# Layer 0 of a four-layer network: images in pairs, one block's planes by halves, another layout of the columns, a new order of steps

## The chip, the cores and the metric

The kernel runs on one core of a Trainium2 chip, as one program. The metric is the device time of one execution in microseconds (us), the median of several runs. The engines named below are TensorE (PE in the profile), VectorE (DVE), ScalarE (ACT), GpSimd (POOL) and SyncE (SP), which issues nearly all DMAs.

## The reference

Four layers run one after the other on a tensor of 32 images of 96 channels and 56 x 56 points, all in float32. Only layer 0 is touched by the change (layer 2 shares a helper with it). Each layer normalises its input over groups of channels (GroupNorm), computes something of it and adds the input back. Layer 0, for one image:

```
xn  = group_norm(x)                              # per image, over groups of channels
h   = silu(bn1(w_exp @ xn))                      # 96 -> 576 channels, 1x1
h   = silu(bn2(depthwise_3x3(h, w_dw)))          # 576 channels
s   = silu(w_se1 @ mean(h) + b_se1)              # 576 -> 24
h   = h * sigmoid(w_se2 @ s + b_se2)             # 24 -> 576, one gate for each channel
y   = x + xn + bn3(w_proj @ h)                   # 576 -> 96, 1x1
```

## The kernel before, in words

**Tiles.** The 96 channels lie on partitions. An image is stored in `xt` as 224 rows of 14 words (`[C, H * NPH, W4]`): each row of 56 points is split into four column phases (point 4q + p has phase p), because layers 1 and 3 want the image so. Three such buffers turn over. The 576 channels of the middle make four and a half blocks of 128. Blocks 0, 1 and 2 (k = 0..2) have their 3x3 convolution on DVE, block 3 ("ab") and the half block 4 ("c", its 64 channels twice on the partitions, one copy for even and one for odd quarters of the image) have it on PE, as nine matmuls with diagonal weights over a padded plane `hpad`.

**Steps.** `run_steps` (L115) goes once through a string `L0_ORDER` (L58 to 63) for each image n and emits the named steps; a suffix + means image n+1, - means n-1, -- means n-2. PE, DVE and ACT run in exactly this order. SP's queue is ordered by the scheduler. The letters:

- s, q: sums of x and of its squared deviation over the image, each one ACTIVATE over 96 x 3136 with an accumulator (L264). u, v: the sum over the group, a small matmul (L270). m, w, b: mean, deviation (POOL's power), bias.
- n: writes the normalised image `xn` with four ACTIVATEs, one for each column phase (L292). `xn` holds even and odd columns apart. r: the residual x + xn, in place in `xt` (L301).
- e k i: expand, block k, quarter i of the image (14 rows): two matmuls of 392 columns, even and odd columns in two PSUM banks, and one eviction by ACT with the first silu into `hpad` (L313). Three PSUM buffers of two banks each ("mm") turn over.
- f k: the first tap of the convolution (ACT, L321); t k 1..8: the other taps (DVE, L326), 24 for an image. z k: second silu (ACT, L332).
- a i (four) and c i (two): the convolutions on PE, `quarters` (L349), with the silu's eviction into `hab` and `hc`.
- g0 to g4: totals (DVE), squeeze (PE, then ACT), excite (PE), gates (DVE, then ACT), gated (DVE): `wg`, the weights of the projection times the gates.
- p i: project, quarter i: for each of two PSUM banks five matmuls, three with `h2` (L407), one with `hab` (L409), one with `hc` (L410). d i: bn and add into `xt` (DVE, L415).
- o: store: statistics of the result for the next layer (eight bn_stats and an aggregate on DVE, L88), six DMAs of the image to DRAM (L425), the fetch of image b+3 into the buffer that comes free (L196), and some copies that prepare layers 1 and 3 ("asides": `twav`, `tdiff`, on SP's queue).

In `project`, bank j holds columns of parity j of the 14 rows, in the order of the rows. `h2` is read with every second column:

```
out = ps[:C, j, :NT]
for k in range(DV):
    nc.tensor.matmul(out.rearrange("c (r w) -> c r w", w=W2), wg[:, k, :],
                     im["h2"][k][:, rows, j::2], start=(k == 0), stop=False)
```

A store writes 3,584 pieces of 56 bytes (14 words) with each of its six DMAs.

Of the kernel before, what the change touches and what calls it, by code (L numbers as in the profile page):

```python
# [10 lines left out]
F32 = mybir.dt.float32  # L11
BF16 = mybir.dt.bfloat16
# [3 lines left out]
ALU = mybir.AluOpType  # L16
# [9 lines left out]
RT = 7  # L26
# [5 lines left out]
PH = HH * NPH  # L32
NP = H // (2 * RT)
PITCH = W + 1
NPAD = (H + 2) * PITCH + 2
PAIRS = C // 2
GR = 16
HALO = 4
# [21 lines left out]
MANUAL = {mybir.EngineType.PE, mybir.EngineType.DVE, mybir.EngineType.Activation}  # L60
MANUAL_SP = MANUAL | {mybir.EngineType.SP}
L0_ORDER = """
    e00 e01 e02 e03 z0- f0 a3- z2- c1- e10 e11 t01 t02 g0- e12 t03 e30 e40 g1- s+ e13 t04 g2- g3-
    e31 e32 t05 e33 g4- t06 t07 u+ f1 m+ t11 p0- p1- q+ t08 d0- v+ w+ p2- t12 e41 d1- p3- d2- t13
    t14 e20 e21 d3- o- b+ t15 e42 t16 e43 e22 e23 f2 a0 t17 t21 a1 n+ t22 t18 t23 t24 t25 t26 t27 r
    z1 t28 c0 a2
"""
L2_ORDER = """
    e00 e10 e11 e12 l3 j0- d0- e01 e20 e02 e21 r u+ e03 e13 j1- m0 e22 d1- e30 m1 e40 v+ j2- d2- e31
# [54 lines left out]
                step[s[0]](image(b), *map(int, s.rstrip("+-")[1:]))  # L124


def padded(pool, nc, n, dtype, name):

    out = []
    for i in range(n):  # L130
        t = pool.tile([128, NPAD], dtype, tag=f"{name}{i}", name=f"{name}{i}")
        nc.gpsimd.memset(t[:, : PITCH + 1], 0.0)
        nc.gpsimd.memset(t[:, PITCH : PITCH * (H + 2) : PITCH], 0.0)
        nc.gpsimd.memset(t[:, PITCH * (H + 1) :], 0.0)
        out.append(t)
    return out

# [12 lines left out]
        nc.sync.dma_start(to, of)  # L150


def tiles(t):

    return t.rearrange("c (t p r) q -> c t p (r q)", t=NP, p=NPH)


def window(t, p, dy, dx, r0, rows):

    at = (r0 + 1 + dy) * PITCH + 1 + dx  # L160
    return t[:p, at : at + rows * PITCH].rearrange("p (r w) -> p r w", w=PITCH)[:, :, 0:W]


@with_exitstack
def layer0(ctx, tc, S, x, w, y0, norm1, tables, aside):

# [20 lines left out]
        return t  # L189

    xs = {}

    def fetch(b):
        if b < B:
            xs[b] = pool.tile([C, H * NPH, W4], F32, tag="xt", name="xt", bufs=3)
            nc.sync.dma_start(xs[b], x[b])  # L196

    fetch(0)
    S.load(nc, w)
# [5 lines left out]
    bse1 = load("l0_bse1", [SEH, 1])  # L205
    wproj = load("l0_wproj", [128, ND + 1, C])
    out4 = load("l0_out", [C, 4])
    fetch(1)
    fetch(2)

    sc, bi = [], []
    for j in range(2):
# [16 lines left out]
    nc.vector.tensor_tensor(bi3, out4[:, 2:3], sc3, ALU.mult)  # L229
    nc.vector.tensor_tensor(bi3, out4[:, 1:2], bi3, ALU.subtract)  # L230

    eye2 = cp.tile([128, HALF], F32, tag="eye2", name="eye2")
    diag = cp.tile([128, 2, 9, HALF], F32, tag="diag", name="diag")
    hpad = padded(cp, nc, 4, F32, "hpad")
    mv_all = cp.tile([C, B, 2], F32, tag="mv0", name="mv0")
    h2s = [cp.tile([128, H, W], F32, tag=f"h2{i}", name=f"h2{i}") for i in range(2)]


    tables()
    nc.vector.tensor_tensor(eye2, S.ident[:, :HALF], S.ident[:, HALF:], ALU.add)  # L240
    for k in (AB, CC):
        for t in range(9):
            nc.vector.tensor_scalar(diag[:, k - AB, t, :], eye2, wdw[:, COL[k], t : t + 1], None, ALU.mult)
    late = ctx.enter_context(tc.tile_pool(name="l0l", bufs=1))
    h2s += [late.tile([128, H, W], F32, tag=f"h2{i}", name=f"h2{i}") for i in (2, 3)]
    hab = late.tile([128, NP, 2, NT], F32, tag="hab", name="hab")
    wg = late.tile([128, ND + 1, C], F32, tag="wg", name="wg")
    h2s.append(late.tile([128, H, W], F32, tag="h24", name="h24"))
    hc = late.tile([128, 2, 2, NT], F32, tag="hc", name="hc")

    ims = {}

    def image(b):

        if b not in ims:
            ims[b] = {
                "b": b, "xt": xs.pop(b), "h2": [None] * DV, "ps": [None] * NP,
                "pad": [hpad[(DV * b + k) % 2] for k in range(DV)] + hpad[2:],
                "ss": sm.tile([128, ND], F32, tag="ss", name="ss"),
            }  # L260
        return ims[b]


    def sums(im, name, func, bias):  # L264
        im[name] = sm.tile([C, 1], F32, tag=name, name=name)
        junk = pool.tile([C, HW], BF16, tag="junk", name="junk", bufs=1)
        nc.scalar.activation(junk, im["xt"].rearrange("c r q -> c (r q)"), func, bias=bias,
                             accum_out=im[name])

    def group_sum(im, name):  # L270
        im["ps" + name] = psm.tile([C, 1], F32, tag="sm", name="pn")
        nc.tensor.matmul(im["ps" + name], S.grp, im[name], start=True, stop=True)

    def mean(im):
        im["nm"] = sm.tile([C, 1], F32, tag="nm", name="nm")
# [16 lines left out]
    def normalise(im):  # L292
        im["xn"] = pool.tile([C, 2, H, W2], F32, tag="xn", name="xn", bufs=1)
        for p in range(NPH):
            nc.scalar.activation(
                im["xn"][:, p % 2].rearrange("c (t r) (q m) -> c m t (r q)", t=NP, m=2)[:, p // 2],
                tiles(im["xt"])[:, :, p], AF.Identity, bias=im["nb"], scale=im["rstd"])

    def residual(im):
# [3 lines left out]
    def expand(im, k, i):  # L303

        c = COL[k]
        rows = slice(2 * i * RT, 2 * (i + 1) * RT)
        ps = psum.tile([128, 2, 512], F32, tag="mm", name="ps")
        for j in range(2):
            nc.tensor.matmul(  # L309
                ps[:, j, :NT], wexp[:, k * 128 : k * 128 + 128],  # L310
                im["xn"][:, j, rows, :].rearrange("c h w -> c (h w)"), start=True, stop=True,
            )
        nc.scalar.activation(  # L313
            window(im["pad"][k], 128, 0, 0, 2 * i * RT, 2 * RT).rearrange("p r (w j) -> p j r w", j=2),
            ps[:, :, :NT].rearrange("p j (r w) -> p j r w", w=W2),
            AF.Silu, bias=bi[0][:, c : c + 1], scale=sc[0][:, c : c + 1],
        )

    def first_tap(im, k):
        im["h2"][k] = h2s[(DV * im["b"] + k) % len(h2s)]  # L320
# [14 lines left out]
    def end_block(im, k):  # L335
        silu2(k, im["h2"][k], im["h2"][k], im["ss"][:, k : k + 1])

    def quarters(k, pad, tiles):


        ps = psum.tile([128, 2, 512], F32, tag="mm", name="psd")
        for t in range(9):
            for j in range(2):
                for r in range(2):
                    c = r ^ j
                    p = slice(r * HALF, (r + 1) * HALF)
                    at = (2 * tiles[r] * RT + t // 3) * PITCH + t % 3
                    v = pad[p, at : at + 2 * RT * PITCH].rearrange("p (r w) -> p r w", w=PITCH)
                    nc.tensor.matmul(  # L349
                        ps[c * HALF : (c + 1) * HALF, j, :NT].rearrange("p (r w) -> p r w", w=W2),  # L350
                        diag[p, k - AB, t, :], v[:, :, j:W:2], start=(t == 0), stop=(t == 8),
                    )
        return ps

# [8 lines left out]
    def depthwise_c(im, i):  # L363

        if i == 0:
            im["hc"] = hc
            im["pc"] = sm.tile([128, 2], F32, tag="pc", name="pc")
        ps = quarters(CC, im["pad"][CC], (2 * i, 2 * i + 1))
        silu2(5, im["hc"][:, i], ps[:, :, :NT], im["pc"][:, i : i + 1])


# [28 lines left out]
    def project(im, i):  # L400
        wg = im["wg"]
        rows = slice(2 * i * RT, 2 * (i + 1) * RT)
        ps = im["ps"][i] = psum.tile([128, 2, 512], F32, tag="mm", name="psj")
        for j in range(2):
            out = ps[:C, j, :NT]
            for k in range(DV):
                nc.tensor.matmul(out.rearrange("c (r w) -> c r w", w=W2), wg[:, k, :],  # L407
                                 im["h2"][k][:, rows, j::2], start=(k == 0), stop=False)
            nc.tensor.matmul(out, wg[:, 3 + j, :], im["hab"][:, i, j, :], start=False, stop=False)  # L409
            nc.tensor.matmul(out, wg[:, 5 + (i % 2 ^ j), :], im["hc"][:, i // 2, j, :], start=False, stop=True)  # L410

    def add(im, i):
        for j in range(2):
            v = tiles(im["xt"])[:, i, j::2]
            nc.vector.scalar_tensor_tensor(  # L415
                v, im["ps"][i][:C, j, :NT].rearrange("c (x m) -> c m x", m=2), sc3, v, ALU.mult, ALU.add)
        if im["b"] == B - 1:
            store_tile(nc, y0, im, i)

    def store(im):  # L420
        b, xt = im["b"], im["xt"]
        channel_stats(nc, sm, xt, mv_all[:, b, :], "t")
        if b < B - 1:
            for to, of in groups(xt, y0, lambda y: y[:, :, b, :], store=True):
                nc.sync.dma_start(to, of)  # L425
        fetch(b + 3)
        if b < B - 4:
            for start in aside[b :: B - 4]:
                start()
        del ims[b]  # L430
# [449 lines left out]
def layer2(ctx, tc, S, k2, y1, y2, norm3):  # L880
# [187 lines left out]
    def store(im):  # L1068
        b = im["b"]
        channel_stats(nc, sm, im["xt"], mv_all[:, b, :], "t")  # L1070
        if b == B - 2:
            for to, of in groups(im["xt"], y2, lambda y: y[:, :, b, :], store=True):
                nc.sync.dma_start(to, of)
        elif b % 2 and b < B - 1:
            for to, of in groups(im["pair"], y2, lambda y: y[:, :, b - 1 : b + 1, :], store=True):
                nc.sync.dma_start(to, of)
            fetch(b + 5)
        del ims[b]

# [289 lines left out]
```

## Time and profile before

| | us |
|---|---|
| median of 3 runs | 6391.51 |
| lowest, highest | 6384.19, 6391.89 |
| the profiled execution | 6501.16 |
| its span | 6499.3 |

The profile describes one execution, and that one was 110 us longer than the median of the runs. The page's first part gives the share of the span for which each engine was busy; layer 0 is about its first half. A few groups of layer 0, from the list of instructions of one round (1800 to 1896 us):

| line | engine, what | count | busy us | mean ns |
|---|---|---|---|---|
| L326 | DVE, tap | 25 | 86.6 | 3480 |
| L349 | PE, depthwise | 432 | 38.5 | 511 |
| L309 | PE, expand | 80 | 27.9 | 497 |
| L313 | ACT, eviction of expand | 20 | 21.4 | 1081 |
| L407 | PE, project with `h2` | 48 | 18.0 | 509 |
| L415 | DVE, add | 8 | 4.6 | 616 |
| L267 | ACT, sums | 2 | 5.7 | 2799, 2909 |

Matmuls overlap in PE's pipeline, so their mean is longer than the distance from one to the next; the busy time is the sum without overlaps. A float32 matmul appears as more than one record.

### The profile page before, as it was taken

The page shows a single profiled execution, that of the slowest core. Times are in us where ns is not written, and L with a number is a line of the kernel's source. Part 1 is how long each engine was busy: PE and PEld are TensorE (multiplying, and loading weights), DVE is VectorE, ACT ScalarE, POOL GpSimd, SP SyncE. Part 2 cuts the span into 40 slices and gives each one's busy share as a digit, 9 for nine tenths or more (in the row PEclk, how much of TensorE's full clock was granted, in tenths as well). Part 3 has the DMA queues.
Part 4 walks back from the last instruction along what each step waited for, and adds up shares of the span by engine and source line. Part 5 has one row for each costly group of instructions (what it writes and reads, how often), then busy time and mean ns, then how long its engine had stood idle before and what let it go on. Part 6 is the DMA issues. An engine that isn't in the chain of part 4 may idle for free.

```text
span 6499.3 us, 115397 instructions
## 1 busy us (share of the span) xinstructions
PE 6025.5 (93%) x49064; PEld 3599.1 (55%) x49064; DVE 5168.3 (80%) x5469; ACT 3953.6 (61%) x5268; POOL 234.1 (4%) x157
## 2 busy tenths in 40 slices
PE   6989989998998998989969999989999999999699
PEld 3444444444444444444535666667777777778344
DVE  8989979898998998989957766657777767676587
ACT  6556555655656565556635565557767766677355
POOL 4000000000000000000000000000000000000000
PEclk8999999999999999989979999999999999999899
DMA  2486475839539439474655776656869695953888
GB/s 80 29 41 50 41 43 41 46 44 40 47 41 41 43 47 42 39 41 39 17 60 143 141 155 150 143 36 45 48 42 50 44 49 41 51 38 31 166 253 248
DMA packets 1631554, 452.94 MB, mean 70 GB/s; under 512 B 1447406, under 2 KB 1625318, under 8 KB 1627582
## 3 DMA queue, kind: packets, MB, share of 16 engines
q1 hardware_dynamic: 1631038, 445.55, 65.7%
q8 instruction: 386, 6.32, 0.6%
q14 instruction: 130, 1.06, 0.1%
HBM read 284.44 MB, written 214.08 MB: 77 GB/s over the span
## 4 chain that ended last, share of the span: by engine, by line
PE 71%; ACT 9%; DMA 9%; SPq 6%; DVE 3%; issue 1%; POOL 1%; ACTq 0%; DVEq 0%
PE psd L349 14%; PE psd L1019 11%; PE ps L309 9%; PE psj L407 8%; PE pc L735 6%; PE ps L1000 5%; SPq L425 4%; DMA y<-xt 4%; PE pc L1175 3%; PE psj L1056 3%; PE psj L409 3%; PE psj L410 2%; ACT hi L972 2%; ACT a L990 2%; DVE h L326 2%; PE pc L719 2%
## 5 line engine op out<-in xcount | busy, mean ns | idle before, releaser
L326 DVE SCALAR_TENSOR_TENSOR h<-hpad,l_wdw,h 128x3136 f32<-128x3136 f32 x768 | 2659.6, 3480 | 28.7 <-ACT h L321 14.9
L349 PE MATMUL psd<-hpad,diag 64*64 64x392 f32 x13824 | 1239.6, 512 | 13.4 <-issue 13.4
L313 ACT ACTIVATE hpad<-ps,o,s 128x784 f32<-128x784 f32 x640 | 684.3, 1081 | 773.3 <-PE ps L309 771.3
L309 PE MATMUL ps<-xn,l_wexp 96*128 96x392 f32 x2560 | 931.6, 516 | 135.6 <-ACT hpad L313 129.1
L1019 PE MATMUL psd<-apad,diag 64*64 64x392 bf16 x20736 | 931.5, 332 | 110.4 <-ACT a L990 57.2
L349 PEld LDWEIGHTS psd<-hpad,diag 64*64 64x64 f32 x13824 | 547.5, 132 | 694.9 <-issue 656.8
L1019 PEld LDWEIGHTS <-diag 64*64 64x64 bf16 x20736 | 695.6, 107 | 342.3 <-issue 164.7
L309 PEld LDWEIGHTS ps<-xn,l_wexp 96*128 96x128 f32 x2560 | 493.4, 197 | 524.2 <-ACT hpad L313 135.3
L565 ACT COPY T<-raw 32x112 f32<-32x112 f32 (+2 forms) x1440 | 462.8, 384 | 308.1 <-DMA raw<-tdiff 223.3
L990 ACT ACTIVATE u<-ps,o,s 128x784 int16<-128x784 f32 x576 | 536.3, 1002 | 162.0 <-PE ps L1000 143.6
L990 ACT ACTIVATE a<-psd,o,s 128x784 int16<-128x784 f32 x448 | 423.7, 999 | 327.7 <-PE psd L1019 327.7
L407 PE MATMUL psj<-h,wg 128*96 128x392 f32 x1536 | 591.4, 520 | 27.9 <-ACT hpad L313 26.4
L1000 PE MATMUL ps<-hi,l_w1q 96*128 96x392 f32 x1280 | 462.4, 361 | 10.0 <-ACT hi L972 9.2
L1175 PE MATMUL pc<-x,T 128*112 128x416 f32 (+1 forms) x1152 | 415.2, 523 | 48.1 <-DMA raw<-tdiff 47.6
L735 PE MATMUL pc<-x,T 128*112 128x416 f32 (+1 forms) x1152 | 445.8, 523 | 0.0
L1000 PE MATMUL ps<-lo,l_w1q 96*128 96x392 f32 x1280 | 438.0, 342 | 0.0
L407 PEld LDWEIGHTS psj<-h,wg 128*96 128x96 f32 x1536 | 249.4, 166 | 289.3 <-issue 258.3
L1175 PEld LDWEIGHTS pc<-x,T 128*112 128x112 f32 x1152 | 204.7, 178 | 258.1 <-issue 240.7
L332 ACT ACTIVATE hab<-psd,o,s 128x392 f32<-128x392 f32 x256 | 170.6, 671 | 263.5 <-PE psd L349 263.5
L332 ACT ACTIVATE h<-h,o,s 128x3136 f32<-128x3136 f32 x96 | 287.9, 2999 | 19.7 <-DVE h L326 19.7
L321 ACT ACTIVATE h<-hpad,l_wdw 128x3136 f32<-128x3136 f32 x96 | 279.1, 2907 | 9.3 <-DMA twav<-zwav 8.3
L735 PEld LDWEIGHTS pc<-x,T 128*112 128x112 f32 x1152 | 190.9, 178 | 143.9 <-issue 143.9
(202 smaller groups left out, 6793.5 us busy)
## 6 DMA issues: line engine op xcount, KB each, us to landing
X<-y SPq DMA_DIRECT2D x192, 392.0 KB
xt<-in_x_dram SPq DMA_DIRECT2D x32, 1176.0 KB
y<-xt SPq DMA_DIRECT2D x192, 196.0 KB
y<-y SPq DMA_DIRECT2D x96, 392.0 KB
xt<-y SPq DMA_DIRECT2D x96, 392.0 KB
out_dram<-y SPq DMA_DIRECT2D x96, 392.0 KB
y<-xt SPq DMA_DIRECT2D x90, 392.0 KB
twav<-zwav SPq DMA_DIRECT2D x768, 36.8 KB
```

Of the source, the lines that this page charges most:

```text
L309: nc.tensor.matmul(ps[:, j, :NT], wexp[:, k * 128 : k * 128 + 128], im["xn"][:, j, rows, :].rearrange("c h w -> c (h w)"), start=True, sto ...
L313: nc.scalar.activation(window(im["pad"][k], 128, 0, 0, 2 * i * RT, 2 * RT).rearrange("p r (w j) -> p j r w", j=2), ps[:, :, :NT].rearrange ...
L326: nc.vector.scalar_tensor_tensor(h2, window(im["pad"][k], 128, t // 3 - 1, t % 3 - 1, 0, H), wdw[:, k, t : t + 1], h2, ALU.mult, ALU.add,)
L332: nc.scalar.activation(view, ps, AF.Silu, bias=bi[1][:, c : c + 1], scale=sc[1][:, c : c + 1], accum_out=accum)
L349: nc.tensor.matmul(ps[c * HALF : (c + 1) * HALF, j, :NT].rearrange("p (r w) -> p r w", w=W2), diag[p, k - AB, t, :], v[:, :, j:W:2], start ...
L407: nc.tensor.matmul(out.rearrange("c (r w) -> c r w", w=W2), wg[:, k, :], im["h2"][k][:, rows, j::2], start=(k == 0), stop=False)
L565: nc.scalar.copy(to.rearrange("x t (p s) -> x t p s", p=NPH), v[:, k])
L735: nc.tensor.matmul(ps[:PH, to], st["T"][j][:, h, k, :], st["x"][:, j, h, of], start=False, stop=(n == NK - 1))
L990: nc.scalar.activation(out, ps, AF.Identity, bias=o[:, c : c + 1], scale=s[:, c : c + 1])
L1000: nc.tensor.matmul(ps[:, j, :NT], w1[:, k * 128 : k * 128 + 128], im[part][:, r0 : r0 + RT, :].rearrange("c h w -> c (h w)"), start=(part ...
L1019: nc.tensor.matmul(ps[q, j, :NT].rearrange("p (r w) -> p r w", w=W), diag[p, k, t, :], v, start=(t == 0), stop=(t == 8))
L1175: nc.tensor.matmul(ps[:, :, to], st["T"][:, h, k, :], st["x"][:, h, :, of], start=(n == 0), stop=(n == NK - 1))
```

## The change

- Images are kept in pairs: two tiles `xt0` and `xt1` of `[C, 224, 2, 14]` take the place of three single ones; an image is a view of one half. The input lies in DRAM in the same pairs. `fetch(b)` is called for even b only and loads images b and b+1; the store of an odd image b calls it for b+3. `store_images` writes images b-1 and b together with six DMAs whose pieces are 112 bytes; images 30 and 31 are still written alone.
- `sums` makes four ACTIVATEs over 96 x 784 into four columns, with a smaller scratch tile, and `group_sum` adds the columns with four accumulating matmuls.
- Block 4's plane `hhalf` has 28 rows: the lower 64 partitions hold rows 0 to 27, the upper ones 28 to 55, each with the neighbour row at the border. Its evictions write 64 partitions, and quarters 1 and 2 have a second, small eviction of one row. Result tile i of c holds quarters i and i + 2.
- Column phases: PSUM bank j of `quarters` and `project` holds phases 2j and 2j+1 (columns 4q + 2j and 4q + 2j + 1). `h2` and the planes are read as pairs of neighbouring words, four words apart. `project` writes its bank with phase 2j first and then phase 2j+1, so that two words that follow each other go to places 196 words apart. `add` then reads the bank straight through and updates 28 rows of 14 words.
- `eye2` lives in `wg`, and the diagonal weights are built after the call of `tables()`.
- A new `L0_ORDER`: step n and e00 to e03, f0 of the next image stand at the end of a round; a3 stands after them; store stands at the start of the second round after its image's (o--, before: o- right behind d3-); s+ is the eighth step of a round.

```diff
-    e00 e01 e02 e03 z0- f0 a3- z2- c1- e10 e11 t01 t02 g0- e12 t03 e30 e40 g1- s+ e13 t04 g2- g3-
-    e31 e32 t05 e33 g4- t06 t07 u+ f1 m+ t11 p0- p1- q+ t08 d0- v+ w+ p2- t12 e41 d1- p3- d2- t13
-    t14 e20 e21 d3- o- b+ t15 e42 t16 e43 e22 e23 f2 a0 t17 t21 a1 n+ t22 t18 t23 t24 t25 t26 t27 r
-    z1 t28 c0 a2
+    z2- c1- o-- t01 g0- e40 g1- s+ t02 e41 e10 e30 g2- e11 t03 u+ g3- e31 e12 t04 e13 g4- f1 t05
+    p0- e32 r t06 m+ q+ p1- t11 d0- t07 d1- t08 z0 t12 p2- d2- p3- e20 t13 d3- v+ w+ e42 e21 e22
+    t14 e23 t15 f2 t16 e33 e43 a0 t21 t17 a1 a2 b+ n+ t22 t23 t18 c0 e00+ e01+ z1 t24 t25 t26 t27
+    e02+ e03+ f0+ a3 t28
...
+def store_images(nc, y, im):
+
+    b = im["b"]
+    if b == B - 2:
+        t, at = im["xt"], b
+    elif b % 2 and b < B - 1:
+        t, at = im["pair"], slice(b - 1, b + 1)
+    else:
+        return
+    for to, of in groups(t, y, lambda y: y[:, :, at, :], store=True):
+        nc.sync.dma_start(to, of)
...
+    pairs = [cp.tile([C, H * NPH, 2, W4], F32, tag="xt0", name="xt0")]
 
     def fetch(b):
+
         if b < B:
-            xs[b] = pool.tile([C, H * NPH, W4], F32, tag="xt", name="xt", bufs=3)
-            nc.sync.dma_start(xs[b], x[b])
+            pair = pairs[b // 2 % 2]
+            nc.sync.dma_start(pair, x[b // 2])
+            for j in range(2):
+                xs[b + j] = pair, pair[:, :, j, :]
...
+    hpad = padded(cp, nc, 3, F32, "hpad") + padded(cp, nc, 1, F32, "hhalf", HH)
...
+        im[name] = sm.tile([C, NP], F32, tag=name, name=name)
+        for i in range(NP):
+            junk = pool.tile([C, 2 * RT * NPH, W4], BF16, tag="junk", name="junk", bufs=1)
+            nc.scalar.activation(junk, im["xt"][:, i * 2 * RT * NPH : (i + 1) * 2 * RT * NPH], func, bias=bias,
+                                 accum_out=im[name][:, i : i + 1])
...
-        nc.tensor.matmul(im["ps" + name], S.grp, im[name], start=True, stop=True)
+        for i in range(NP):
+            nc.tensor.matmul(im["ps" + name], S.grp, im[name][:, i : i + 1], start=(i == 0), stop=(i == NP - 1))
...
+        parts = [(slice(128), 2 * i * RT, slice(2 * RT))]
+        if k == CC:
+            lo, up = slice(64), slice(64, 128)
+            parts = [(up if i // 2 else lo, i % 2 * 2 * RT, slice(2 * RT))]
+            parts += [[], [(up, -1, slice(2 * RT - 1, 2 * RT))], [(lo, HH, slice(1))], []][i]
...
+    def phases(v, j):
+
+        return v.rearrange("p r (q j m) -> p j r q m", j=2, m=2)[:, j]
...
-                        ps[c * HALF : (c + 1) * HALF, j, :NT].rearrange("p (r w) -> p r w", w=W2),
-                        diag[p, k - AB, t, :], v[:, :, j:W:2], start=(t == 0), stop=(t == 8),
+                        ps[c * HALF : (c + 1) * HALF, j, :NT].rearrange("p (r q m) -> p r q m", q=W4, m=2),
+                        diag[p, k - AB, t, :], phases(v[:, :, :W], j), start=(t == 0), stop=(t == 8),
...
-        ps = quarters(CC, im["pad"][CC], (2 * i, 2 * i + 1))
+        ps = quarters(CC, im["pad"][CC], (i, i))
...
-            out = ps[:C, j, :NT]
+            out = ps[:C, j, :NT].rearrange("c (m r q) -> c r q m", m=2, q=W4)
+            hab, hc = (im[n].rearrange("p i j (r q m) -> p i j r q m", q=W4, m=2) for n in ("hab", "hc"))
             for k in range(DV):
-                nc.tensor.matmul(out.rearrange("c (r w) -> c r w", w=W2), wg[:, k, :],
-                                 im["h2"][k][:, rows, j::2], start=(k == 0), stop=False)
-            nc.tensor.matmul(out, wg[:, 3 + j, :], im["hab"][:, i, j, :], start=False, stop=False)
-            nc.tensor.matmul(out, wg[:, 5 + (i % 2 ^ j), :], im["hc"][:, i // 2, j, :], start=False, stop=True)
+                nc.tensor.matmul(out, wg[:, k, :], phases(im["h2"][k][:, rows], j), start=(k == 0), stop=False)
+            nc.tensor.matmul(out, wg[:, 3 + j, :], hab[:, i, j], start=False, stop=False)
+            nc.tensor.matmul(out, wg[:, 5 + (i // 2 ^ j), :], hc[:, i % 2, j], start=False, stop=True)
...
-            v = tiles(im["xt"])[:, i, j::2]
+            n = 2 * i + j
+            v = im["xt"][:, 2 * n * 2 * RT : 2 * (n + 1) * 2 * RT, :]
             nc.vector.scalar_tensor_tensor(
-                v, im["ps"][i][:C, j, :NT].rearrange("c (x m) -> c m x", m=2), sc3, v, ALU.mult, ALU.add)
+                v, im["ps"][i][:C, j, :NT].rearrange("c (r q) -> c r q", q=W4), sc3, v, ALU.mult, ALU.add)
...
-        channel_stats(nc, sm, xt, mv_all[:, b, :], "t")
-        if b < B - 1:
-            for to, of in groups(xt, y0, lambda y: y[:, :, b, :], store=True):
-                nc.sync.dma_start(to, of)
-        fetch(b + 3)
+        b = im["b"]
+        channel_stats(nc, sm, im["xt"], mv_all[:, b, :], "t")
+        store_images(nc, y0, im)
+        if b % 2:
+            fetch(b + 3)
```

## The prediction

> **What bounds the kernel now.** First the slices of the page (40 slices of 162 us). Layer 0 fills the first 20 or so.
>
> ```profile
> PE   6989989998998998989969999989999999999699
> DVE  8989979898998998989957766657777767676587
> ACT  6556555655656565556635565557767766677355
> PEclk8999999999999999989979999999999999999899
> ```
>
> TensorE is the busiest engine there, VectorE (DVE) close behind, ScalarE (ACT) far from full; but both leading engines dip in the same slices. So I listed who waits in 100 to 2900 us (us in total, times, longest):
>
> ```profile
> ACT junk L267 <- DMA xt<-in_x_dram: 138.6, 7, 27.0
> DVE wg L397 <- ACT gate L393: 136.1, 7, 26.6
> PEld ps L309 <- ACT hpad L313: 132.0, 7, 26.6
> PE ps L309 <- ACT hpad L313: 127.0, 7, 26.0
> ```
>
> These are seven events, each seen four times: the sums of image n+1 (step s) wait on ACT for their fetch, the evictions behind them leave TensorE without a free PSUM buffer, and the gates behind those hold DVE. Next, stretches with and without such an event (columns: PE, PEld, DVE, ACT, POOL busy, then clock, DMA share, GB/s):
>
> ```profile
> 1800.00:1896.00 96.00, 94.59 (x620) 47.08 (x619) 92.36 (x52) 61.68 (x63) 3.63 (x1) 1.00 0.36 47
> 1896.00:1992.00 96.00, 94.59 (x620) 47.11 (x619) 92.38 (x52) 61.72 (x63) 3.63 (x1) 1.00 0.60 44
> 1505.00:1620.00 115.00, 92.34 (x601) 45.69 (x600) 89.08 (x48) 62.13 (x62) 1.42 (x1) 0.88 1.38 30
> ```
>
> A clean round is all TensorE: 94.6 of 96 us, and nothing but shorter TensorE work could shorten it. The start of step s in the timeline of ACT goes from 142.8 us (image 2) to 3119.1 us (image 31): 2976.3 us in 29 rounds, mean 102.6, while clean ones take 96.35. The excess is 2976.3 - 29 x 96.35 = 182 us. Last, why a fetch is late, in SP's own timeline (start, duration):
>
> ```profile
> 695.06 30.68 SPq L425 DMA_DIRECT2D y<-xt  x6
> ...
> 735.89 0.32 SPq L196 DMA_DIRECT2D xt<-in_x_dram  x1
> ...
> 793.16 57.21 SPq L425 DMA_DIRECT2D y<-xt  x6
> ...
> 871.15 0.34 SPq L196 DMA_DIRECT2D xt<-in_x_dram  x1
> ```
>
> The fetch reuses the stored buffer, so it waits for the store. Mostly that takes 41 us, but for images 2, 6, 9, 13, 18, 22, 25 and 29 the six stores of 56-byte pieces last 66 to 76 us to the last packet. Layer 2 stores pairs, 112-byte pieces, and each of its 15 stores looks like this one, with 40 to 42 us to the last packet:
>
> ```profile
> 4731.53 33.37 SPq L1076 DMA_DIRECT2D y<-xt  x6
> ```
>
> **What the Trainium skill says.** "DMA: Bandwidth & Descriptors", Specifications, wants at least 512 B per transfer for line rate. The trace agrees in kind: twice the bytes in layer 2's pair store took no longer than a single image's. "TensorE: Matmul & The Clock Gate", What's actually happening, says that an idle window of about 3.4 us halves the clock; the trace shows 0.88 in the stretch with a stall and 1.00 in the clean ones, so a stall costs a little more than its length. "PSUM — Partial Sum Buffer", Specifications, has 8-byte lines and says that any non-contiguous pattern slows matmuls significantly; no row of before writes single words apart. "SBUF — State Buffer", Specifications, wants two hits per 16-byte line; the old stride-2 reads and the new pairs both give two.
>
> **The change, part by part.**
>
> *Pairs.* Stores become 15 of the layer 2 kind and two singles at the end. I take layer 2's 40 to 42 us for all of them, so the slow ones go, and with them up to 182 us. But three single buffers become two pairs: a fetch is issued once in two rounds, in the round whose step s needs it. Two things hold it. The store of the pair begins when step d3- ends. Let P be the end of p3- on TensorE; d3- ends at P+1.4, the last packet is out at about P+45. And the fetch comes after o--'s eight bn_stats, which now stand behind 13 taps: 13 x 3.48 us on DVE brings t28 to P+47.4, and eight bn_stats with the aggregate (3.83 + 0.37) to P+51.6. SP has one aside copy (twav) between store and fetch, no more; behind the waiting fetch stand the copies that prepare layers 1 and 3, for which nothing in layer 0 waits. A single fetch lands 7 us after issue, two queued together at the start of the kernel took 13, so the pair is there at about P+64.7.
>
> When is it wanted? On TensorE after p3-: e20, v+, 6 e, a0 a1 a2, c0, 4 e+, a3. With e at 1.315 us, one depthwise call (quarters) at 6.38, this is about P+47; c1- ends at 53.5, e40 at 54.8. ACT does z2-, c1- and e40 by 56.0, squeeze's silu by 56.4, and then stands at s+. So it waits about 8.3 us. Behind it queue the evictions of e41, e10 and e30; TensorE has three PSUM buffers, fills them, and stops at e11. That is 14 rounds (images 4, 6, ... 30), each 8.3 us plus about 1 us of half clock. With a store that ended later the wait would grow only beyond P+51.6: that is the cover.
>
> *Sums in quarters.* Four ACTIVATEs of 784 (about 1.0 us each from the rows of that size) with an accumulator read of 0.19 for one of 2.80: ACT has room, +1.5 us twice a round. Group sums take four matmuls for one: three more at 0.11 us, twice, 0.7 us of TensorE per round.
>
> *Halves of block 4.* Same number of matmuls. Evictions on 64 partitions are no shorter than on 128; two small ones (64 x 56) add about 0.2 us each on ACT, hidden under TensorE. Memsets and the diagonals, now built later, are in the prologue.
>
> *Column phases, reads.* 432 depthwise and 48 project passes a round read pairs in place of every second word. Stride-2 reads pitch at 345 to 352 ns, contiguous ones at 329. Bounds: 0, or what separates them, 23 ns on each of 108 groups of depthwise matmuls and 16 ns on each of 48 project passes: 3.2 us a round. A loss has no bound from the trace; the skill's two hits per line, which stay, speak against one. I take 0.
>
> *Column phases, writes.* 80 passes of project per image write words 196 apart. Bound below 0: no reason excludes a small gain. Bound above: twice the pass, 80 x 0.33 = 26 us a round. The nearest rows: bf16 passes of 392 pitch at 165 ns, fp32 ones at 329, so a float pass with one word per line would ask for as many PSUM lines per ns as the bf16 one already gets (1.2). I take 0. The add reads PSUM contiguously now: layer 2's does, at 618 ns against 616, so 0.
>
> *Order.* Per round TensorE has 94.8 + 0.7 = 95.5 us of work. Laid out by hand with these durations, it waits 0.8 us for the totals (g0- behind t01 on DVE), 0.6 to 1.3 for e41's eviction behind s+, and about 0.7 elsewhere: 97.6 us (to 98.5), against 96.35. At 95 us of work DVE is just covered.
>
> *Prologue.* The first fetch is two images, image 0 is there 6 us later. The tail stays.
>
> **The sum**, against the profiled execution: 15 rounds x 97.6 + 14 x (97.6 + 9.3) = 1464 + 1497 = 2961; 2961 - 2976 + 6 = -10 us on its 6499.3 us of span. The median of the runs, 6391.5, is 110 us below that execution (6501.2); I carry the difference over as it is: 6381, rounded to 6380. What a measurement of this kernel tells from no change is about 0.2%, 13 us.
>
> **The rivals.** A is this sum: the slow stores are traded for a wait in every other round. Range 6335 (stall 5 us in place of 8.3) to 6430 (rounds of 98.5, stall 10). Chance 0.42: 0.22 faster, 0.10 the same, 0.10 slower.
>
> B, the wait is mostly hidden: the fetch of a pair takes less than 13 us, ACT reaches s+ later than laid out, or pair reads are cheaper (3.2 x 29 = 93 us). With a stall of 2 us: 15 x 97.6 + 14 x 99.8 = 2861, and -109 in all: 6280. For it speaks that the fetch's two parts (7 and 13 us) come from a start with other loads in flight; against it that DVE, full as it is, can't bring o-- forward. Chance 0.26.
>
> C, the scattered PSUM writes cost. At 0.1 us a pass 8 us a round, 6640; at twice the pass 7200. For it speaks the skill's page, against it the line rate. Chance 0.12.
>
> D, slower: the late fetches are to a good part the profiled execution's own. It is 110 us longer than the median, and the 56-byte stores are what varies in it. The gain is the excess that timed runs have; the costs (15 x 1.25 + 14 x 10.55 + 6 = 172 us) stay. It decides from an excess below 172. If all 110 us were missing, 72 would be left: 6391 + 100 = 6490; half of it gives 6435. For it speaks that nothing else in layer 0 varies; against it that layers 1 to 3 move most of the data and may hold the difference. Chance 0.20, of which 0.18 slower.
>
> **How the numbers follow.** Faster: 0.22 + 0.26 = 0.48; the same 0.10 + 0.02; slower 0.10 + 0.18 + 0.12 = 0.40. The likeliest is A, 6380. A range for 8 in 10 takes in A, most of B (to 6265) and D to 6500, and leaves C out.
>
> **What would show it.** In the new trace: pair stores all near 41 us; step s waiting for its fetch 14 times for about 8 us, and in between no wait on a DMA; the project passes' mean unchanged near 510 to 520 ns; rounds alternating between about 98 and 107 us. A mean of project well above 520 is C. Even rounds above 99 mean that the order leaves more holes than I laid out. No waits of s+ mean B.

## The result, and the profile after

The changed kernel takes 6550.06 us (median of 4 runs, 6541.39 to 6563.87), the kernel before 6389.99 us: a ratio of 1.0254, with a 95% interval of 1.0235 to 1.0273. It is 160 us slower. The profiled execution of the changed kernel has a span of 6562.0 us.

First the waits of the changed kernel in 100 to 3000 us (us in total, times, longest):

```profile
ACT junk L287 <- DMA xt<-in_x_dram: 100.3, 13, 8.5
PEld ps L330 <- ACT hhalf L342: 117.8, 28, 9.1
PE ps L330 <- ACT hhalf L342: 115.4, 28, 9.0
DVE wg L431 <- ACT gate L427: 143.5, 28, 10.3
```

The seven long waits for a fetch have become thirteen of about 8 us, in every other round (a fourteenth, of 9.0 us, lies behind this window). Here is one of them, first on SP, then on DVE, then on ACT (start, duration). The step p3- of this round ended at 2176.6 us; this is P.

```profile
2177.84 33.44 SPq L162 DMA_DIRECT2D y<-xt  x6
2227.74 0.34 SPq L211 DMA_DIRECT2D xt<-in_x_dram  x1
```

```profile
2216.95 7.01 DVE L355 SCALAR_TENSOR_TENSOR h<-hpad,l_wdw,h 128x3136 f32<-128x3136 f32 x2
2223.87 3.84 DVE L87 BATCH_NORM_STATS2 stt<-xt 96x6 f32<-96x392 f32 x8
2227.74 0.37 DVE L88 BATCH_NORM_AGGREGATE mv<-stt 96x2 f32<-96x48 f32 x1
```

```profile
2232.81 0.23 ACT L415 ACTIVATE s1g<-pse,l_bse 24x1 f32<-24x1 f32 x1
2240.90 0.86 ACT L287 ACTIVATE junk<-xt 96x784 bf16<-96x784 f32 x1 [7.86 <-DMA xt<-in_x_dram]
```

The fetch goes out at P+51.1, in the moment in which the eight bn_stats end, and not when the pair's store has been issued (P+34.7). ACT is free at P+56.4 and gets the pair at P+64.3.

Second, one short and one long round by the windows view (PE, PEld, DVE, ACT, POOL busy, clock, DMA share, GB/s), and four slices of 4 us in the short one:

```profile
1968.30:2076.90 108.60, 100.24 (x634) 49.94 (x633) 92.54 (x51) 64.94 (x76) 3.63 (x1) 0.92 0.37 67
2076.90:2176.60 99.70, 99.19 (x634) 49.09 (x633) 92.52 (x51) 64.94 (x76) 3.63 (x1) 0.97 0.05 15
2134.90:2138.90 4.00, 3.49 (x19) 2.41 (x18) 3.96 (x4) 3.90 (x9) 0.00 (x0) 1.00 0.00 0
2138.90:2142.90 4.00, 4.00 (x13) 2.60 (x12) 3.50 (x3) 3.37 (x4) 0.00 (x0) 0.52 0.00 0
2142.90:2146.90 4.00, 4.00 (x9) 2.26 (x8) 3.08 (x2) 3.25 (x5) 0.00 (x0) 0.63 0.00 0
2146.90:2150.90 4.00, 4.00 (x13) 2.00 (x12) 3.96 (x2) 3.74 (x3) 0.00 (x0) 1.00 0.00 0
```

TensorE is busy for 99.2 of the short round's 99.7 us and waits for 0.5; clean rounds of before had 94.6 of 96. Part of the difference is the clock: it falls to half at P+62 although TensorE has work. The clock's records in the trace show a half-clock stretch at that place in every one of the 27 rounds that I counted, 324 us of them in all: 6.8 us in 12 of the 14 short rounds and 10.2 in two, 17.1 us in the long ones, where the wait for the pair stands in front of it. TensorE's timeline shows what stands there in the short round:

```profile
2136.58 1.49 PE L420 MATMUL pg<-s1g,l_wse 24*128 24x1 f32 x12
2138.58 2.58 PE L330 MATMUL ps<-xn,l_wexp 96*128 96x392 f32 x4 [0.51 <-ACT hhalf L342]
2140.95 1.33 PE L293 MATMUL pn<-s,grp 96*96 96x1 f32 x8
2142.14 5.04 PE L330 MATMUL ps<-xn,l_wexp 96*128 96x392 f32 x9
```

Excite's twelve one-column records (a matmul shows as two), a wait of half a microsecond, the first four expand passes, eight one-column records of the group sum; and then nine passes of expand in 5.04 us, which take 3 us at full clock.

What the column phases cost is seen in the instructions of the same short round:

```profile
L383 PE MATMUL psd<-hpad,diag 64*64 64x392 f32 x288 | 25.8, 511 | 0.0
L442 PE MATMUL psj<-h,wg 128*96 128x392 f32 x48 | 17.9, 506 | 0.0
L450 DVE SCALAR_TENSOR_TENSOR xt<-psj,sc,xt 96x392 f32<-96x392 f32 x8 | 4.6, 616 | 4.0 <-PE psj L444 4.0
```

Before, the depthwise matmul, project with `h2` and the add took 511, 509 and 616 ns: the phases cost nothing.

### The profile page after: what moved, and what is told of

Same layout as the page of the kernel before. It is cut to its first block, busy times and chain, and to the rows that moved or that the text cites. A ratio compares the mean times of both kernels' runs of the same rounds, so it can differ in the third digit from the quotient of the medians.

```text
span 6562.0 us, 116352 instructions
## 1 busy us (share of the span) xinstructions
PE 6129.5 (93%) x49448; PEld 3678.3 (56%) x49448; DVE 5159.4 (79%) x5469; ACT 4045.6 (62%) x5716; POOL 225.4 (3%) x157
## 4 chain that ended last, share of the span: by engine, by line
PE 72%; DVE 12%; ACT 8%; DMA 5%; issue 1%; POOL 1%; SPq 1%; ACTq 0%; DVEq 0%; POOLq 0%
PE psd L1053 11%; DVE h L355 10%; PE psd L383 10%; PE ps L330 9%; PE psj L442 8%; PE ps L1034 6%; PE pc L769 6%; PE pc L1205 6%; PE psj L1090 3%; DMA xt<-in_x_dram 3%; PE psj L443 3%; PE psj L444 3%; ACT hi L1006 2%; ACT junk L287 2%; PE pc L753 2%; ACT a L1024 2%
## 5 line engine op out<-in xcount | busy, mean ns | idle before, releaser
L330 PE MATMUL ps<-xn,l_wexp 96*128 96x392 f32 x2560 | 1021.5, 551 | 160.3 <-ACT hhalf L342 130.1
L1053 PEld LDWEIGHTS <-diag 64*64 64x64 bf16 x20736 | 713.0, 108 | 340.7 <-issue 176.2
L330 PEld LDWEIGHTS ps<-xn,l_wexp 96*128 96x128 f32 x2560 | 523.4, 211 | 562.8 <-issue 142.5
L342 ACT ACTIVATE hpad<-ps,o,s 128x784 f32<-128x784 f32 x512 | 543.0, 1075 | 463.0 <-PE ps L330 460.3
L383 PE MATMUL psd<-hpad,diag 64*64 64x392 f32 x9216 | 825.5, 511 | 0.0
L383 PEld LDWEIGHTS psd<-hpad,diag 64*64 64x64 f32 x9216 | 353.3, 131 | 461.4 <-issue 461.0
L442 PE MATMUL psj<-h,wg 128*96 128x392 f32 x1536 | 573.4, 508 | 2.7 <-DVE wg L431 1.5
L383 PE MATMUL psd<-hhalf,diag 64*64 64x392 f32 x4608 | 416.5, 509 | 0.0
L1205 PEld LDWEIGHTS pc<-x,T 128*112 128x112 f32 x1152 | 204.7, 178 | 245.8 <-issue 225.4
L383 PEld LDWEIGHTS psd<-hhalf,diag 64*64 64x64 f32 x4608 | 178.3, 131 | 227.0 <-issue 227.0
```

The costliest lines, as they stand in the source:

```text
L330: nc.tensor.matmul(ps[:, j, :NT], wexp[:, k * 128 : k * 128 + 128], im["xn"][:, j, rows, :].rearrange("c h w -> c (h w)"), start=True, sto ...
L342: nc.scalar.activation(window(im["pad"][k][p], p.stop - (p.start or 0), 0, 0, r0, n).rearrange("p r (w j) -> p j r w", j=2), ps[p, :, :NT] ...
L383: nc.tensor.matmul(ps[c * HALF : (c + 1) * HALF, j, :NT].rearrange("p (r q m) -> p r q m", q=W4, m=2), diag[p, k - AB, t, :], phases(v[:, ...
L442: nc.tensor.matmul(out, wg[:, k, :], phases(im["h2"][k][:, rows], j), start=(k == 0), stop=False)
L1053: nc.tensor.matmul(ps[q, j, :NT].rearrange("p (r w) -> p r w", w=W), diag[p, k, t, :], v, start=(t == 0), stop=(t == 8))
L1205: nc.tensor.matmul(ps[:, :, to], st["T"][:, h, k, :], st["x"][:, h, :, of], start=(n == 0), stop=(n == NK - 1))
```

## The experiments

All times below are medians, and each ratio is to the kernel before, run on the same chip with it. The chips were not the same throughout, and the kernel before took 6380 to 6387 us beside the experiments and 6390 beside the changed kernel; so a few microseconds between versions on different chips say nothing.

**The kernel before once more.** No edit. The profile on which I had built the sum was an execution 110 us above the median, so I wanted another one.

> The kernel before, unchanged, for a second profile of it. Theory 1 (its late fetches belong to the kernel): again seven or eight stores of 66 to 76 us, about 180 us of excess over 96.35 us rounds in layer 0, and an execution near 6500. Theory 2 (they belong mostly to that one profiled execution): an execution near 6390 with some 70 to 90 us of excess, three or four late fetches.

Measured: 6389.58 us, ratio 1.0005 (0.9996 to 1.0014); the span of its profiled execution is 6393.5 us. Its waits in 100 to 2900 us:

```profile
ACT junk L267 <- DMA xt<-in_x_dram: 58.0, 7, 9.8
PEld ps L309 <- ACT hpad L313: 51.1, 7, 9.4
PE ps L309 <- ACT hpad L313: 45.6, 7, 8.8
DVE wg L397 <- ACT gate L393: 55.6, 7, 9.4
```

The same seven fetches of the same images are late, but each by less: 4.8 to 9.8 us where the first profile had 11.6 to 27.0. For the store of image 6 and the fetch behind it, SP's timeline has:

```profile
776.27 45.60 SPq L425 DMA_DIRECT2D y<-xt  x6
837.25 0.34 SPq L196 DMA_DIRECT2D xt<-in_x_dram  x1
```

Step s of image 2 to step s of image 31 takes 2881.8 us, which is 88 us above 29 rounds of 96.35, not 182. Theory 2 had the size right and the number of late fetches wrong: the late fetches do belong to the kernel, but more than half of their length (138.6 us against 58.0) belonged to that execution. Its slow stores of 56-byte pieces were longer (57.21 us of issue for image 6 against 45.60 here); why, no run here shows.

**The store earlier.** In the order of the changed kernel the store goes right behind d3-:

```diff
-    z2- c1- o-- t01 g0- e40 ...
+    z2- c1- t01 g0- e40 ...
-    ... e20 t13 d3- v+ w+ ...
+    ... e20 t13 d3- o- v+ w+ ...
```

> The changed kernel with one step moved: the store (bn_stats, then the pair's fetch) stands right behind d3- instead of two rounds' starts later. Theory 1 (the wait for the pair in every other round is made by the eight bn_stats behind 13 taps): the pair lands about P+55 to P+58 in place of P+64, step s waits 0 to 2 us, the long rounds come from 108.6 to about 101, time about 6550 - 14 x 7 = 6450. Rival (the wait is the store's own length and the fetch's): the wait stays at 5 us or more and the time within 40 us of 6550.

Measured: 6443.78 us, ratio 1.0098 (1.0068 to 1.0128), 106 us less than the changed kernel.

```profile
2113.27 33.23 SPq L162 DMA_DIRECT2D y<-xt  x6
2154.31 0.34 SPq L211 DMA_DIRECT2D xt<-in_x_dram  x1
```

The fetch now goes out 41.0 us after the store, when the store has landed, and step s waits at most 1.8 us (6.0 us in all). So the place of the bn_stats made the wait. The rounds, though, are 99.7 to 102 us: the half-clock stretch in every round has stayed.

**Single images, four buffers.** The changed kernel with four single images in place of two pairs, stored as before in 56-byte pieces:

```diff
-            pair = pairs[b // 2 % 2]
-            nc.sync.dma_start(pair, x[b // 2])
+            xs[b] = singles[b % 4]
+            nc.sync.dma_start(xs[b], x[b])
...
-        if b % 2:
-            fetch(b + 3)
+        fetch(b + 4)
```

> The changed kernel with four single image buffers in place of two pairs (56-byte stores again, fetch of image b+4), order as changed. Every fetch then has a round of slack. Theory 1: all rounds near 99.7 us, no wait of step s, 6550 - 14 x 9 = 6425. Rival (56-byte stores disturb by more than late fetches, so that pairs are needed): 6480 or more.

Measured: 6438.23 us, ratio 1.0087 (1.0067 to 1.0107). No fetch is late at all, though the stores are the short-pieced ones, and rounds are 99.7 to 102 us. A round of slack does as much as pairs with an early store; what remains above the kernel before is not the fetch.

**The order of before in the changed kernel.** Only the string is exchanged.

> The changed kernel with the order of steps of before, everything else as changed. If the order is what lost (theory 1: the short rounds are 3.3 us longer because small matmuls stand together and the clock is halved after them, the long ones because of the late store step), rounds go to about 97 to 98 us, time 6390 to 6430. If the pairs, the halves or the column phases lose by themselves (rival), it stays above 6480.

Measured: 6387.74 us, ratio 1.0002 (0.999 to 1.0014). Pairs, halves, split sums and column phases together neither gain nor lose. Inside, they do both: no fetch is late and the 29 rounds take 2868.8 us (13 less than before), but step s of image 2 stands at 160.2 us, where it stood at 143.0 before. And the rounds do not become the clean ones of before, with 96.3 us; here are two:

```profile
1882.20:1981.70 99.50, 97.77 (x634) 48.34 (x633) 92.84 (x52) 64.90 (x76) 3.63 (x1) 0.98 0.40 72
1981.70:2079.40 97.70, 97.48 (x633) 48.27 (x632) 92.73 (x51) 64.98 (x76) 3.63 (x1) 0.98 0.05 16
```

Together the 29 rounds are 75 us above 29 clean ones, so most of the 88 us that the kernel before loses there is lost again in another way. An estimate from this trace covers it: 96 us at half clock, in 24 stretches, cost about 48, and the larger group sums 1.0 us a round (1.5 us of TensorE against 0.5), which is 29. No run takes the two apart.

**The new order in the kernel before.** The reverse: only the string, with three single buffers.

> The kernel before with the new order of steps, nothing else of the change. Its fetch is a single image, issued at P+51 in every round, and lands about P+58.5. Theory 1 (the order is what loses, and pairs make its late store step worse): a wait of step s of 1 to 3 us in every round, the half-clock stretch in every round, rounds of 99 to 101 us, 6400 to 6460: between both kernels. Rival (the order only loses together with the split sums and halves): 6390 or less.

Measured: 6483.4 us, ratio 1.0147 (1.012 to 1.0173): more than I had expected. One short round, one long:

```profile
1931.50:2030.90 99.40, 98.22 (x622) 48.98 (x621) 92.59 (x51) 62.04 (x62) 3.63 (x1) 0.97 0.43 44
2030.90:2140.20 109.30, 99.27 (x622) 49.53 (x621) 92.58 (x51) 61.93 (x62) 3.63 (x1) 0.92 1.00 40
```

Step s waits about 2 us in every round, as expected, and 11 to 14 us where the 56-byte store is slow, which I had left out: the later the fetch, the more a slow store shows. So the order costs 98 us on the old buffers (6386 to 6483) and 162 us on the new ones (6388 to 6550).

**One group-sum matmul.**

```diff
-        im["ps" + name] = psm.tile([C, 1], F32, tag="sm", name="pn")
-        for i in range(NP):
-            nc.tensor.matmul(im["ps" + name], S.grp, im[name][:, i : i + 1], start=(i == 0), stop=(i == NP - 1))
+        pn = psm.tile([C, NP], F32, tag="sm", name="pn")
+        nc.tensor.matmul(pn, S.grp, im[name], start=True, stop=True)
+        im["ps" + name] = sm.tile([C, 1], F32, tag="ps" + name, name="pt")
+        nc.vector.tensor_reduce(im["ps" + name], pn, AX.X, ALU.add)
```

> The changed kernel with one group-sum matmul over four columns in place of four accumulating ones, and a small reduce on DVE behind it. Theory 1 (the four small matmuls cost 1.6 us a round themselves, and the thin stretch on TensorE that they make with squeeze and excite halves the clock for 6.8 us, which costs another 3.4): short rounds go from 99.7 to 97 or 98 and half-clock stretches become fewer than one a round; 6470 to 6510. Rival (thin matmuls only cost their own time): 1.3 us a round, half-clock stretches as before, 6510 to 6520.

Measured: 6523.9 us, ratio 1.0215 (1.0185 to 1.0244): 26 us less than the changed kernel, which misses both forecasts by 4 to 14 us. Short rounds are 97.0 to 98.7 us in place of 99.7, but the start of layer 0 is 12 us longer (step s of image 2 at 169.3 us in place of 157.2), and a half-clock stretch is still there in all 27 rounds, often shorter. Fewer thin matmuls do not take it away.

**One group-sum matmul, with the order of before.** The same edit, and the string of `old_order`.

> The changed kernel with the order of before and one group-sum matmul in place of four: no late fetch, no extra small matmuls. Theory 1: rounds of 96.4 to 97.5 us, 29 x 1.5 us below the version with the old order alone: 6340 to 6360, under both kernels. Rival (what the thin matmuls gave up comes back as the wait of the project on the silu that it already shows in some rounds): 6370 or more.

Measured: 6384.55 us, ratio 1.0003 (0.9991 to 1.0014): the forecast is missed and the rival holds. The 29 rounds take 2861.9 us, 7 less than with the old order alone, and the start 11 us more (step s of image 2 at 171.6 us). In 300 to 2900 us TensorE waits 53.6 us for the evictions in front of project, where it waited 38.7 with the old order alone.

**The first group sum later.** The same instructions, one of TensorE's steps moved:

```diff
-    ... g2- e11 t03 u+ g3- e31 e12 t04 e13 g4- ...
+    ... g2- e11 t03 g3- e31 e12 t04 e13 u+ g4- ...
```

> The changed kernel with one step moved on TensorE: the first group sum (u+) stands behind e13 in place of between excite and the next expands. Same instructions. Theory 1 (the cluster squeeze, excite, group sum and the wait at e11 halves the clock in every round): shorter half-clock stretches, 1 to 2 us less a round, 6490 to 6520. Rival (the clock is halved by squeeze, excite and the wait alone): 6540 to 6560.

Measured: 6484.04 us, ratio 1.0158 (1.0135 to 1.018): 66 us less than the changed kernel, more than expected. A short round, and TensorE's timeline at the same place of it:

```profile
2040.30:2137.50 97.20, 95.88 (x633) 47.17 (x633) 92.43 (x51) 64.54 (x76) 3.63 (x1) 1.00 0.05 15
```

```profile
2099.95 1.50 PE L420 MATMUL pg<-s1g,l_wse 24*128 24x1 f32 x12
2101.96 5.53 PE L330 MATMUL ps<-xn,l_wexp 96*128 96x392 f32 x16 [0.51 <-ACT hhalf L342]
2107.33 0.76 PE L293 MATMUL pn<-s,grp 96*96 96x1 f32 x8
```

Sixteen passes of expand in 5.53 us, at the full clock; the wait of 0.51 us in front of them is the same. Half-clock stretches fell from 27 to 15, and but for two short ones they are in the long rounds, whose wait of about 8 us has stayed. So the group sum's place is worth time. It does not start the half clock, though: in the changed kernel's short round the clock is down 2 us before the first matmul of the group sum, at 2140.95 us:

```profile
2136.95:2138.95 2.00, 1.49 (x12) 1.33 (x12) 2.00 (x4) 1.96 (x5) 0.00 (x0) 1.00 0.00 0
2138.95:2140.95 2.00, 2.00 (x4) 0.94 (x3) 2.00 (x2) 1.64 (x2) 0.00 (x0) 0.52 0.00 0
```

In front of the fall stand squeeze (4.5 us before excite), excite and the wait of 0.51 us; which of them it takes, no run separates. What the place of the group sum decides can be read from the clock's records of the nine kernels that have pairs or four buffers and this order, in the 190 rounds without a wait of over 0.7 us behind excite. Where the clock fell, it stayed at half for 6.8 or 10.2 us in all 64 rounds with the four matmuls within 5 us of excite's start, and for 3.4 us in all 56 with the group sum 7 us or more behind it. One matmul in place of four, near excite, gave 6.8 us nine times and 3.4 us six times.

Whether the clock falls is another matter. In each of these traces it changes only at points of a grid of 3.413 us (off by less than 0.01 us). It fell in every round that had such a point 1.7 to 3.7 us behind excite's start, and in none whose nearest points were at 0.6 to 1.6 and 4.0 to 5.0 us; in between it did both. All 15 short rounds of the changed kernel have a point in the first range, because a short and a long round together take 208.2 us, 61 steps of the grid. With the later group sum they settle at 204.8 us, 60 steps, and only 3 of 15 short rounds have one there. So a part of the 66 us is luck with the length of the rounds.

**Both moves.**

> The changed kernel with both moved steps: the store behind d3-, and the first group sum behind e13. If the two losses are separate (theory 1), their gains add: 6550 - 106 - 66 = 6378, rounds of 97.3 to 98.5 us, half-clock stretches in few rounds. If they are one loss seen twice (rival: in both cases what was gained is the half clock after the stall), little is gained beyond the better one of the two: 6430 to 6445.

Measured: 6378.54 us, ratio 0.9996 (0.9983 to 1.0008). The gains of 106 and 66 us add, as theory 1 said; that they meet its 6378 to the microsecond is luck, as the interval is 8 us to either side. A pair's wait is 1.1 us at most; of half clock 65 us are left, in 16 stretches. In the round of one of them sixteen passes of expand take 7.23 us, where they took 5.53 in the version above, all of them before the group sum:

```profile
2026.44 1.49 PE L420 MATMUL pg<-s1g,l_wse 24*128 24x1 f32 x12
2028.45 7.23 PE L330 MATMUL ps<-xn,l_wexp 96*128 96x392 f32 x16 [0.51 <-ACT hhalf L342]
2035.51 0.76 PE L293 MATMUL pn<-s,grp 96*96 96x1 f32 x8
```

The early store alone has 222 us of half clock in 300 to 2900 us, both moves have 65, and only the place of the group sum differs: this pair of kernels is the cleanest measure of it, 65 us (6443.78 to 6378.54), though the share of the grid is in it too.

**A start in smaller pieces.** The first fetch as four DMAs by rows:

```diff
-            nc.sync.dma_start(pair, x[b // 2])
+            n = NP if b == 0 else 1
+            for i in range(n):
+                rows = slice(i * H * NPH // n, (i + 1) * H * NPH // n)
+                nc.sync.dma_start(pair[:, rows], x[b // 2][:, rows])
```

> As the version with both moved steps, and the first fetch, images 0 and 1 together, issued as four DMAs by rows, so that each quarter of step s waits for its own rows. Theory: step s of image 0 starts 3 to 5 us earlier, and the time is 3 to 5 us below the other version, under both kernels. Rival (the start is set by weights and constants of the prologue): the same time.

Measured: 6369.38 us, ratio 0.9979 (0.9964 to 0.9993): the first version under the kernel before, by 0.2%. Step s of image 2 stands at 151.1 us, 6 us earlier than in the version with both moves (157.1).

**The diagonals early.** In addition, the diagonal weights are built ahead of `tables()`, from a corner of the first `h2` tile.

> The version with both moved steps and the split first fetch, and the diagonal weights built before the tables, as in the kernel before (their identity in a corner of the first h2 tile). Theory: the first depthwise matmul waits for the diagonals that stand behind the tables' DMAs (they are built at 103 us in the changed kernel, at 21 us before), so the start of layer 0 gains 8 to 14 us: 6355 to 6362. Rival (the start is bound by the larger first fetch alone): 6365 to 6372.

Measured: 6366.43 us, ratio 0.9976 (0.9966 to 0.9985). The first depthwise matmul starts 16.9 us earlier and step s of image 2 4 us earlier (146.7), but the time can't be told from the version without it (0.9979): the rival's range, 6365 to 6372, is what came.

**Early diagonals and one group-sum matmul.**

> As the version with early diagonals, and one group-sum matmul over four columns with a small reduce in place of four matmuls. Theory (small matmuls cost their own 1.0 to 1.6 us of TensorE a round): 20 to 40 us less. Rival (TensorE then waits as much longer for the evictions or for the sum's chain through DVE): within 10 us of it.

Measured: 6379.26 us, ratio 0.9999 (0.9991 to 1.0007): 13 us more than without, beyond the rival's bound by a little. The TensorE time saved came back: project now waits at its beginning for the gated weights (14 times) or for an eviction (12 times), at most 1.1 and 1.3 us. The likely reason is argued and not shown: the group sum is now followed by a reduce on DVE, behind a tap of 3.5 us.

## Why the prediction was wrong, step by step

Forecast was 6380, measured 6550. From one profile to the other (6393.5 to 6562.0, the second profile of before) the 168 us lie in: 142 in the 29 rounds, 14 at the start of layer 0, 8 in its last round, 4 elsewhere. The sum had -10, so 178 us have to be explained: 94 by the reference, 63 by the rounds, 8 each by start and last round, 4 by the rest.

- **The sum's reference was the step that failed most.** I took 2976 us for the rounds of before and carried the difference to the median "as it is". The execution behind the median has 2882: 94 us of the gain that I booked for ending slow stores were not there to be gained. The rival D had this mechanism, its place and its threshold (an excess below 172 us; it was 88) and 0.20 of the chance. A profile that lies 110 us off the median should have made D the forecast, or the sum should have been made with both references. Even D gave 6490 at most; the 60 us above it are costs that the sum had too small, in the rounds above all.
- **The pair's wait was right.** P+56.4 and P+64.7 were forecast, P+56.4 and P+64.3 measured; the cover that I named (the bn_stats behind 13 taps) is what the experiment with the early store moved. Its price of 9.3 us a long round measures 8.9 (108.6 against 99.7).
- **Short rounds: too small.** 97.6 us forecast (to 98.5), 99.7 measured. TensorE was to work for 95.5 us and to wait for 2.1; it worked for 99.2 and waited for 0.5, so that the work was 3.7 us too small and the waits, 1.6 us too large, hid a part of that by luck. The group sums cost 1.6 us a round and not 0.7 (16 records take 2.1 us, 4 took 0.5; at full clock, in the version with the old order, 16 take 1.5). And I had put half clock at nothing except behind the long waits: it comes in every round (expand's passes take 31.1 us in a short one, 27.4 and 27.7 in clean rounds of the two profiles of before). It could have been seen in the kernel before: in its second profile nine rounds without a late fetch have it as well, and those with 6.8 us of it last 98.1 us in place of 96.3. Over 15 short and 14 long rounds this is 63 us (3024 measured from step s to step s, 2961 forecast).
- **Start and end: 14 and 8 us** where I had 6 and 0. The start was the size of the first fetch, by 6 us (split fetch), and the late diagonals by 4; the rest of it, and what adds 8 us to the last round, was not tried.
- **Column phases: right.** C is out: project's passes, which write words 196 apart, take 506 ns against 509, depthwise 511 against 511, the add 616 against 616. A price of 0 for reads and writes is what the trace shows.
- **Pair stores: right.** 33.4 us of issue, none slow. Sums in quarters: ACT goes from 62.1 to 64.9 us a round, hidden, as forecast. (The two small evictions of block 4 are in it; they take 0.40 us each and not 0.2.)

The change's own purpose, to end slow stores, is reached, but is worth 13 us in the rounds with the old order, where the late fetches had seemed to promise 88; the start, 17 us longer, takes these 13 back. The new order of steps loses 98 to 162 us.

## What to carry to other kernels

Before a gain is worked out from waits in a profile, compare that execution's time with the median of the runs: waits on DMAs may be half as long in the others. When a buffer is freed by a reader, look at what stands in front of that reader on its engine; eight cheap bn_stats behind thirteen taps cost 106 us. Steps of thin matmuls on TensorE are better kept apart, with full matmuls between them: the group sum behind three more expands was worth 65 us. And before a gain is put down to such a move, look at whether the length of the round has changed which rounds the clock's grid hits.

## What the hardware showed that I had not expected

- TensorE's clock was halved while TensorE had work: in the 3.41 us in front of the fall at 2138.97 us TensorE counts as busy for 2.90, with excite's twelve one-column records and one wait of 0.5 us among them. The stretch was 6.8 us long in 13 of 15 short rounds. With the group sum 3 us later it is gone from 12 of 15 short rounds and 3.4 us long in the others.
- The clock's changes lie on a grid of 3.413 us in each trace (stretches last 3.4, 6.8, 10.2, 13.7, 17.1 us and so on), so whether a short thin place on TensorE costs anything depends on where in the grid it falls.
- Single-precision project passes into PSUM with words that follow each other 784 bytes apart ran as fast as contiguous ones (506 and 509 ns); the Trainium skill's "PSUM — Partial Sum Buffer", Specifications, says that any non-contiguous pattern slows matmuls significantly. The measurement decides: not this one.
- Stores of 56-byte pieces were slow for the same eight images in all four profiles of kernels that have them, with three buffers or four: 51 to 57 us of issue in the first profile of before, 42 to 47 in the other three, where the other stores take 26 to 32. Pairs, 112 bytes a piece, take 32 to 35 us every time.
